# A two-layer graph network: the table stage's weights loaded beside the experts' last steps, and the score products behind a branch

## The chip, the cores and the metric

The kernel runs on one core of one Trainium2 chip. The metric is the device time of one execution in microseconds (us), and the time of a kernel is the median of several runs.

## The reference

A graph has 3125 nodes of 256 features, 100,000 edges and eight types of edge. Two layers follow one another. Each adds to the node features x three things: a message-passing network over the edges, a linear attention over all nodes, and a mixture of experts of which each node uses two. What matters here, cut from the reference (`act` stands for the exact gelu, `ln` for a normalization without weights):

```python
# layer 0, the experts: E = 8, hidden size 1024
logits = xt @ Wr + br
top_p, top_idx = jax.lax.top_k(softmax(logits), 2)
h = act(einsum('end,edh->enh', ln(xt) * ln_g + ln_b, W1) + b1)
y = einsum('enh,ehd->end', h, W2) + b2
x = x + (weights * y_of_the_two).sum(axis=1)
...
# layer 1, the network over the edges: R = 8 types, 8 heads of 32
xn = ln(x)
h_all = einsum('nf,rof->rno', xn, W)                 # a table of R * N rows
scores = einsum('ehd,hd->eh', h_all[type, src], attn_src) \
       + einsum('ehd,hd->eh', h_all[type, dst], attn_dst)
...
# layer 1, the attention: keys and values
k, v = ln_k(heads(xn @ wk.T)), ln_v(heads(xn @ wv.T))
kv = einsum('bhsd,bhse->bhde', k, v) / N
```

The scores are linear in h_all, so the kernel multiplies the attention vectors into the weights once: a small matrix `score_w` (256 rows, 2 × 8 × 8 columns) gives both halves of every score from xn itself.

## The kernel before, in words

The work is one program, `fast` (line 2117), whose stages follow one another. The nodes lie in 25 tiles of 128.

**Layer 0** up to line 2277: adjacency, linear attention, two rounds of aggregation, then the router (`tokens`, its logits added at line 1901) and the plan that scatters each node's rows to the experts (`plan`, scatters of rows at line 1951).

**The experts** (`experts`, line 2017) make 30 steps of 256 rows, s = 0 to 29. `fetch(s + 1)` at the head of step s issues seven loads on the SP queue: the rows fx (line 2036), four small ones (2040 to 2043), and the two halves of the expert's weights, fw1 and fw2 (2045, 2047), 1 MB each, two buffers each. Then come the first product fhp (2072) with the gelu on ACT (2073), the turn of the next step's rows (ftp, 2056, and fxe, 2058), the second product fyp (2080), the bias (2082), the store of the rows (2083, on ACT's queue), and `beside(s)` (2282), which does a share of other work. In the experts `tc.manual_schedule(engines=ORDERED)` holds: TensorE (PE), VectorE (DVE) and ScalarE (ACT) execute in written order, whereas SP and GpSimd (POOL) are placed by the scheduler.

In `beside`, step 16 loads the layer-1 weights wn on POOL's queue (line 2286, 8 loads of 256 KB). At step 22 it calls `score_weights` (2087): six small DVE operations build at_w (2092, 2098), 32 products of wn with at_w go to TensorE (sp, line 2106; each float32 product is two records, so 64), and four DVE copies (2109, 2111) bring them to score_w. After step 29 a branch (`tc.If`, 2311) holds two seldom steps more. It isn't taken with these inputs.

**The table stage** (2318 to 2411) is scheduled freely on all engines. Ahead of its loop are the loads of its weights on SP: wq, wo (line 353 in `load_k`), wt (2 MB), wkv, bo, kg and kb (2330 to 2337), and a row of padding (2339 to 2341). For each node tile t it gathers two rows y per node from the experts' output (POOL, 2351; three buffers each), adds them to xs (DVE, 2354), takes mean and variance (2356, 2357), a square root on ACT and a reciprocal (2358, 2359), normalizes to x (338), and turns it: tp on TensorE (345), copied to xt on ACT (346). From xt come four products hp of 128 × 512 columns with wt (2371; 16 records), copied to the table's stage by ACT for even j (2376) and by DVE for odd j (2374); the scores ap (2379, 2380) with score_w; and kvp (2389), whose normalization (2392 to 2405) leads to kv (2408). The two PSUM buffers of hp are used in turn, so product j + 2 waits for the copy of product j.

**Layer 1** (`Layer1`, line 1145) then walks over the edges by blocks: gathers of table rows (r, line 1404) and sums (line 1493). Its order is written out by hand.

Pools of SBUF tiles are stacks of addresses. A tile that lies where another lay before waits for the last use of that one. Loads and stores issued on SP and ACT signal through eight semaphores in rotation, so an issue waits for the landing of the transfer eight before it.

Of the kernel before, what the change touches and what calls it, by code (L numbers as in the profile page):

```python
# [8 lines left out]
F32 = mybir.dt.float32  # L9
BF = mybir.dt.bfloat16  # L10
I32 = mybir.dt.int32
AF = mybir.ActivationFunctionType
OP = mybir.AluOpType
# [2002 lines left out]

def experts(tc, C, T, a, pool, wp, wk, ps, beside, first, steps):
# [69 lines left out]
def score_weights(nc, C, a, late, f, wn, blk_p):  # L2087
# [6 lines left out]
    for i, name in enumerate(("L1_gnn_attn_srcc", "L1_gnn_attn_dstc")):  # L2094
        col = f.tile([P, 2], F32, name=f"att{i}")
        nc.sync.dma_start(col, a[name])
        for oc in range(2):
            nc.vector.tensor_scalar(at_w[:, oc, i * HD:(i + 1) * HD], head[:, oc, :],
                                    col[:, oc:oc + 1], None, op0=OP.mult)

# [16 lines left out]
def fast(ctx: ExitStack, tc: tile.TileContext, a, out, flag):  # L2117
# [153 lines left out]


    with tc.tile_pool(name="blk", bufs=1) as blk, tc.tile_pool(name="blk_p", bufs=1, space=PSUM) as blk_p, \
            tc.tile_pool(name="f", bufs=1) as f:
        B_ = Blocks(nc, late, dram, blk, a, places)

        score_w = None
        wn = f.tile([P, R, 2, D], F32, name="wn")
# [3 lines left out]
        def beside(s):  # L2282
            nonlocal score_w
            if s == 16:
                for r in range(R):
                    tc.keep_in_program_order(nc.gpsimd.dma_start(
                        wn[:, r], a["L1_gnn_W"][r].rearrange("(k p) n -> p k n", p=P)))
            if s == 22:
                score_w = score_weights(nc, C, a, late, f, wn, blk_p)
# [17 lines left out]
        with tc.tile_pool(name="fw", bufs=2) as fw, tc.tile_pool(name="fk", bufs=3) as fk, \  # L2307
                tc.tile_pool(name="fp", bufs=2, space=PSUM) as fp:
            with tc.manual_schedule(engines=ORDERED):
                experts(tc, C, T_, a, f, fw, fk, fp, beside, 0, NE0 + NT - SELDOM)  # L2310
        with tc.If(nc.values_load(T_.over[0:1, 0:1], min_val=0, max_val=1) > 0):
            with tc.tile_pool(name="fw_l", bufs=2) as fw, tc.tile_pool(name="fk_l", bufs=3) as fk, \
                    tc.tile_pool(name="fp_l", bufs=2, space=PSUM) as fp:
                with tc.manual_schedule(engines=ORDERED):
                    experts(tc, C, T_, a, f, fw, fk, fp, lambda s: None, NE0 + NT - SELDOM, NE0 + NT)


    with tc.tile_pool(name="n1", bufs=1) as n1:
        apart = dram.tile([NB, P, 3, HD * R], BF, name="apart")
        x1t = dram.tile([(NB + 3) // 4, P, 2, 512], F32, name="x1t")  # L2320
        cx = n1.tile([P, 2, P], F32, name="cx1")
        wq = load_k(nc, n1, a["L1_mix_wqT"], "wq")
        wo = load_k(nc, n1, a["L1_mix_woT"], "wo")
        with tc.tile_pool(name="r", bufs=1) as r1, tc.tile_pool(name="rw", bufs=3) as rw, \
                tc.tile_pool(name="rc", bufs=1, space=PSUM) as rc, \
                tc.tile_pool(name="rp", bufs=2, space=PSUM) as rp:
            wt = load_k(nc, r1, a["L1_gnn_WT"], "wt")
            wkv = r1.tile([P, 2, 2 * D], F32, name="wkv")
            for i, name in enumerate(("L1_mix_wkT", "L1_mix_wvT")):
                nc.sync.dma_start(wkv[:, :, i * D:(i + 1) * D], a[name].rearrange("(k p) n -> p k n", p=P))  # L2330
            bo = r1.tile([P, D], F32, name="bo")
            nc.sync.dma_start(bo, row_bc(a["L1_mix_bo"], D))
            kg = r1.tile([P, 2, 64], F32, name="kg")
            kb = r1.tile([P, 2, 64], F32, name="kb")
            for i, c in enumerate("kv"):
                nc.sync.dma_start(kg[:, i, :], row_bc(a[f"L1_mix_ln_{c}_g"], 64))
                nc.sync.dma_start(kb[:, i, :], row_bc(a[f"L1_mix_ln_{c}_b"], 64))
            pad = r1.tile([1, TW], F32, name="pad")
            nc.vector.memset(pad[:, :D], 0.0)
            nc.vector.memset(pad[:, D:], FAR)  # L2340
            nc.sync.dma_start(tab2[PADTAB:PADTAB + 1, :], pad)

            st = r1.tile([P, NB, 6], F32, name="st_x2")
            mv = r1.tile([P, NB, 2], F32, name="mv_x2")
            rs = r1.tile([P, NB], F32, name="rs_x2")
            cps = [rc.tile([P, P], F32, name=f"kv{g}") for g in range(2)]
            rows = tab2[:R * NP, :].rearrange("(r t p) c -> t p r c", r=R, p=P)
            for t in range(NB):
                for i in range(2):
                    y = rw.tile([P, D], F32, name=f"y{i}")  # L2350
                    nc.gpsimd.indirect_dma_start(  # L2351
                        out=y, out_offset=None, in_=T_.y,
                        in_offset=bass.IndirectOffsetOnAxis(ap=T_.back[:, i * NB + t:i * NB + t + 1], axis=0))
                    nc.vector.scalar_tensor_tensor(xs[:, t, :], y, T_.wt[:, i, t:t + 1], xs[:, t, :],
                                                   op0=OP.mult, op1=OP.add)
                nc.vector.bn_stats(st[:, t, :], xs[:, t, :])
                nc.vector.bn_aggr(mv[:, t, :], st[:, t, :])
                nc.scalar.activation(rs[:, t:t + 1], mv[:, t, 1:2], AF.Sqrt, bias=C.eps)
                nc.vector.reciprocal(rs[:, t:t + 1], rs[:, t:t + 1])
                x1 = rw.tile([P, D], F32, name="x1")  # L2360
                normal(nc, x1, xs[:, t, :], mv, rs, t)
                nc.vector.tensor_add(xs[:, t, :], xs[:, t, :], bo)
                xt = rw.tile([P, 2, P], F32, name="xt1")
                transposed(nc, C, rp, xt, x1)
                nc.sync.dma_start(x1t[t // 4][:, :, t % 4 * P:(t % 4 + 1) * P], xt)

                stage = rw.tile([P, R, TW], F32, name="stage")
                for j in range(R // 2):
                    hp = rp.tile([P, 2, D], F32, name="hp", tag="a")
                    for k in range(2):  # L2370
                        nc.tensor.matmul(hp.rearrange("p r d -> p (r d)"), xt[:, k, :],  # L2371
                                         wt[:, k, j * 512:(j + 1) * 512], start=(k == 0), stop=(k == 1))
                    if j % 2:
                        nc.vector.tensor_copy(stage[:, 2 * j:2 * j + 2, :D], hp)
                    else:
                        nc.scalar.copy(stage[:, 2 * j:2 * j + 2, :D], hp)
                ap = rp.tile([P, 2 * R * HD], F32, name="ap", tag="b")
                for k in range(2):
                    nc.tensor.matmul(ap, xt[:, k, :], score_w[:, k, :], start=(k == 0), stop=(k == 1))
                nc.vector.tensor_copy(stage[:, :, D:], ap[:, :R * HD].rearrange("p (r h) -> p r h", r=R))  # L2380
                a3 = rw.tile([P, 3, HD * R], BF, name="a3")
                bf_parts(nc, rw, a3[:, 0, :], a3[:, 1, :], a3[:, 2, :], ap[:, R * HD:], [P, HD * R])
                nc.sync.dma_start(apart[t], a3)
                nc.sync.dma_start(rows[t], stage)

                n = P if t < NB - 1 else LAST
                kvp = rp.tile([P, 8, 64], F32, name="kvp", tag="b")
                for k in range(2):
                    nc.tensor.matmul(kvp.rearrange("p h d -> p (h d)"), xt[:, k, :], wkv[:, k, :],  # L2389
                                     start=(k == 0), stop=(k == 1))  # L2390
                mean = rw.tile([P, 8], F32, name="mean")
                nc.vector.tensor_reduce(mean, kvp, AX.X, OP.add)
                nc.vector.tensor_scalar(mean, mean, 1.0 / 64, None, op0=OP.mult)
                kv = rw.tile([P, 8, 64], F32, name="kv")
                nc.vector.tensor_tensor(kv, kvp, mean[:, :, None].to_broadcast([P, 8, 64]), OP.subtract)
                sq = rw.tile([P, 8, 64], F32, name="sq")
                nc.scalar.activation(sq, kv, AF.Square)
                var = rw.tile([P, 8], F32, name="var")
                nc.vector.tensor_reduce(var, sq, AX.X, OP.add)
                nc.scalar.activation(var, var, AF.Sqrt, bias=C.eps, scale=1.0 / 64)  # L2400
                nc.vector.reciprocal(var, var)
                nc.vector.tensor_tensor(kv, kv, var[:, :, None].to_broadcast([P, 8, 64]), OP.mult)
                kv4 = kv.rearrange("p (i h) d -> p i h d", i=2)
                nc.vector.tensor_tensor(kv4, kv4, kg[:, :, None, :].to_broadcast([P, 2, 4, 64]), OP.mult)
# [75 lines left out]
```

## Time and profile before

| what | value |
| --- | --- |
| three runs, us | 3027.10, 3026.31, 3028.59 (median 3027.1) |
| the profiled execution | 3027.1 us, of which its span on the core 3025.3 |
| mean granted TensorE clock | 0.916 of full speed |
| busy share of the span | PE 83%, DVE 61%, POOL 33%, ACT 24% |
| moved by DMA | 416.82 MB, mean 138 GB/s |
| step of the experts away from `beside`'s larger shares | 14.31 us |
| table stage, first gather to last kv | 1377.6 to 1653.5 us |

The span runs from the first instruction to the last. In lines of the profile, PE is TensorE's matmuls and PEld its weight loads, which overlap them. A line of the timeline has the start and the length of a run of equal instructions, then engine, source line, operation, output <- inputs, shape and count; the bracket tells how long the engine sat idle before and what ended it. "SPq" and "ACTq" are instructions that issue transfers. In a row of windows, each engine has its busy time in the stretch and, in brackets, its number of instructions. The granted clock is the share of full speed that TensorE was given.

### The profile page before, as it was taken

To read this page: it belongs to the slowest core of one execution; us is meant where nothing else is said; L and a number is where in the kernel's file an instruction comes from. 1 tells how busy PE (TensorE), PEld (TensorE's weight loads), DVE (VectorE), ACT (ScalarE), POOL (GpSimd) and SP (SyncE) were. 2 spreads that over 40 slices of the span, in tenths; PEclk is the share of its full clock that TensorE was granted. 3 is DMA by queue.
4 is the path that set the end of the run, shared out by engine and by line. 5 is a ranking of instruction groups with operands and counts; after the bars stand their busy time and mean duration, and the time that the engine had idled before them with its cause. 6 is when DMAs were issued, how large, how long until landed. Compare 5 with 4: busy or idle time off the path is not lost.

```text
span 3025.3 us, 37763 instructions
## 1 busy us (share of the span) xinstructions
PE 2522.7 (83%) x13349; PEld 1720.9 (57%) x13349; DVE 1842.2 (61%) x4082; ACT 735.1 (24%) x1646; POOL 997.2 (33%) x1040
## 2 busy tenths in 40 slices
PE   2788799999978999997998565977877977969788
PEld 1556554455557888883444444555555654655556
DVE  7999787756562111116866577657667766676652
ACT  3444212222232222222322111212121212112122
POOL 2000000002224600005101777765747656666500
PEclk9899999999988999898999777998989887988999
DMA  3333356533334666455434555544535445455412
GB/s 111 73 73 76 105 185 210 190 95 109 93 118 153 225 196 198 147 171 181 152 124 140 161 139 152 152 139 129 166 100 160 142 119 150 132 148 142 121 42 89
DMA packets 383645, 416.82 MB, mean 138 GB/s; under 512 B 143189, under 2 KB 318298, under 8 KB 383188
## 3 DMA queue, kind: packets, MB, share of 16 engines
q1 hardware_dynamic: 313454, 266.28, 28.9%
q0 software_dynamic: 49072, 132.49, 15.5%
q10 hardware_dynamic: 20918, 15.51, 1.7%
q8 instruction: 109, 1.79, 0.2%
q14 instruction: 92, 0.75, 0.1%
HBM read 316.18 MB, written 97.96 MB: 137 GB/s over the span
## 4 chain that ended last, share of the span: by engine, by line
PE 29%; DVE 9%; POOL 6%; DMA 5%; issue 4%; ACT 2%; DVEq 0%; ACTq 0%; SPq 0%; POOLq 0%
PE sums L1493 8%; PE hp L1285 7%; POOL r L1404 6%; PE hp L2371 5%; PE yp L1337 4%; DMA r<-tab,b_at 3%; DVE r L1479 1%; PE kvp L2389 1%; DVE oh L1482 1%; PE dp L1229 1%; PE yp L1596 1%; DMA y<-route_y,slot 1%; DMA ew<-in_L_ffn_expert_w 1%; DVE xs L1341 1%; ACT h L1288 0%
## 5 line engine op out<-in xcount | busy, mean ns | idle before, releaser
L1404 POOL DMA_INDIRECT r<-tab,b_at x831 | 801.4, 964 | 603.0 <-issue 228.5
L1493 PE MATMUL sums<-r,oh 128*128 128x264 f32 x1662 | 417.5, 407 | 46.6 <-DVE oh L1482 24.2
L1493 PEld LDWEIGHTS sums<-r,oh 128*128 128x128 f32 x1662 | 330.0, 201 | 127.4 <-issue 30.3
L1951 POOL DMA_INDIRECT route_x<-x,slot x50 | 50.6, 1012 | 811.9 <-DVE slot L1947 644.2
L1479 DVE TENSOR_TENSOR r<-r,fixed 128x1792 f32<-128x1792 f32 (+2 forms) x123 | 239.5, 1947 | 3.4 <-ACT fixed L1467 3.4
L2072 PE MATMUL fhp<-fxe,fw 128*128 128x256 f32 x960 | 219.5, 387 | 0.9 <-DVE fxe L2058 0.6
L2222 PE MATMUL agg<-at,px 128*128 128x512 bf16 (+2 forms) x1050 | 217.2, 358 | 2.2 <-DMA row_g<-in_L_gnn_g 2.2
L1337 PE MATMUL yp<-ew,h 128*128 128x256 f32 x600 | 162.3, 422 | 66.8 <-DVE xs L1341 59.7
L2222 PE MATMUL agg<-at,py 128*128 128x512 bf16 (+4 forms) x1200 | 217.9, 335 | 0.0
L1288 ACT ACTIVATE h<-hp,bc 128x512 f32<-128x512 f32 (+2 forms) x168 | 106.2, 639 | 450.5 <-PE hp L1285 450.5
L2080 PE MATMUL fyp<-fw,fhid 128*128 128x256 f32 x960 | 212.2, 379 | 0.0
L2072 PEld LDWEIGHTS fhp<-fxe,fw 128*128 128x128 f32 x960 | 176.3, 193 | 38.6 <-ACT fhid L2073 6.6
L2080 PEld LDWEIGHTS fyp<-fw,fhid 128*128 128x128 f32 x960 | 180.3, 190 | 23.2
L1285 PE MATMUL hp<-xt,ew 128*128 128x512 f32 (+2 forms) x336 | 166.7, 624 | 22.1 <-ACT h L1288 13.0
L2371 PE MATMUL hp<-wt,xt 128*128 128x512 f32 x400 | 180.7, 601 | 3.2 <-ACT xt L346 2.7
L1229 PE MATMUL dp<-a,ot 128*128 128x64 bf16 x2493 | 111.2, 208 | 85.5 <-DVE own L1240 43.8
L1337 PEld LDWEIGHTS yp<-ew,h 128*128 128x128 f32 x600 | 122.5, 212 | 101.8 <-DVE xs L1341 66.7
L2073 ACT ACTIVATE fhid<-fhp,fb 128x256 f32<-128x256 f32 x240 | 113.5, 473 | 270.7 <-PE fhp L2072 254.8
L1229 PEld LDWEIGHTS <-ot 128*128 128x128 bf16 x2493 | 106.2, 108 | 108.7 <-issue 50.3
L2351 POOL DMA_INDIRECT y<-route_y,slot x50 | 51.2, 1025 | 350.4 <-DVE pad L2340 325.3
L2222 PEld LDWEIGHTS <-py 128*128 128x128 bf16 (+1 forms) x1200 | 111.5, 99 | 88.1 <-issue 5.5
L2222 PEld LDWEIGHTS <-px 128*128 128x128 bf16 (+1 forms) x1050 | 96.3, 98 | 105.4 <-issue 10.3
(423 smaller groups left out, 3841.3 us busy)
## 6 DMA issues: line engine op xcount, KB each, us to landing
fw<-in_L_ffn_W SPq DMA_DIRECT2D x60, 1024.0 KB
ew<-in_L_ffn_expert_w SPq DMA_DIRECT2D x126, 256.0 KB
at<-adj SPq DMA_DIRECT2D x44, 640.0 KB
route_x<-zero SPq DMA_DIRECT2D x104, 256.0 KB
tab<-stage SPq DMA_DIRECT2D x25, 1056.0 KB
oe<-b_order SPq DMA_DIRECT2D x97, 256.0 KB
adj<-adj_o SPq DMA_DIRECT2D x78, 250.0 KB
r<-tab,b_at POOLq DMA_INDIRECT x831
```

The source lines that it names most:

```text
L1229: nc.tensor.matmul(dp[:, i, :, :].rearrange("p h r -> p (h r)"), ot[:, i * P:(i + 1) * P], A["a3"][:, j, :], start=(j == 0), stop=(j == 2))
L1285: nc.tensor.matmul(hp[:, :W], ws[i, e][:, n, j * P:(j + 1) * P], x[:, n, :W], start=(n == 0), stop=(n == 1))
L1288: nc.scalar.activation(o[:, j, :W], hp[:, :W], AF.Relu, bias=b[:, e, j:j + 1])
L1337: nc.tensor.matmul(yp, h2[e][:, n, i * P:(i + 1) * P], ws[3, e][:, n, :], start=(n == 0), stop=(n == 1))
L1404: st = self.nc.gpsimd.indirect_dma_start(out=r[:, c, :], out_offset=None, in_=self.table, in_offset=bass.IndirectOffsetOnAxis(ap=self.B.at ...
L1479: nc.vector.tensor_tensor(rv, rv, self.factors[:, s0:s0 + k, :, None].to_broadcast([P, k, HD, DH]), OP.mult)
L1493: mm = nc.tensor.matmul(self.sums, oh[:, c, :], r[:, c, :], start=(i == 0), stop=(i == w - 1))
L2072: nc.tensor.matmul(hp, w1[:, k, i * P:(i + 1) * P], xe[:, k, :], start=(k == 0), stop=(k == 1))
L2073: nc.scalar.activation(hid[:, i, :], hp, AF.Gelu, bias=b1[:, 0, i:i + 1])
L2080: nc.tensor.matmul(yp, hid[:, i, t * P:(t + 1) * P], w2[:, i, :], start=(i == 0), stop=(i == K1 - 1))
L2222: nc.tensor.matmul(agg[g][:, :cw], parts[j][:n, k, g * P:(g + 1) * P], at[:n, i, :cw], start=(k == 0 and j == 0), stop=(k == NB - 1 and j ...
L2371: nc.tensor.matmul(hp.rearrange("p r d -> p (r d)"), xt[:, k, :], wt[:, k, j * 512:(j + 1) * 512], start=(k == 0), stop=(k == 1))
```

## The change

A new function `table_weights` makes the tiles of the table stage's weights in pools that are opened before the experts, and a generator of six portions of loads on SP. `beside` draws one portion at each step from 24 on: a quarter of wt (512 KB) at steps 24 to 27; wkv and bo at 28; kg, kb, wq and wo at 29. `score_weights` is split: `score_columns` builds at_w at step 22, and the products and copies stand after the branch. wn and at_w move to a pool that lives until the table stage ends. A square root of one column, `root`, stands on ACT at the experts' end. The rest of the table stage keeps its text, with one level of indentation less.

```diff
+def table_weights(tc, a, n1, r1):
+    nc = tc.nc
+    wq, wo = (n1.tile([P, 2, D], F32, name=n) for n in ("wq", "wo"))
+    wt = r1.tile([P, 2, R * D], F32, name="wt")
+    wkv = r1.tile([P, 2, 2 * D], F32, name="wkv")
+    bo = r1.tile([P, D], F32, name="bo")
+    kg, kb = (r1.tile([P, 2, 64], F32, name=n) for n in ("kg", "kb"))
+    def loads():
+        split = lambda name: a[name].rearrange("(k p) n -> p k n", p=P)
+        keep = lambda o, i: tc.keep_in_program_order(nc.sync.dma_start(o, i))
+        for x in range(0, R * D, 512):
+            keep(wt[:, :, x:x + 512], split("L1_gnn_WT")[:, :, x:x + 512])
+            yield
+        for i, name in enumerate(("L1_mix_wkT", "L1_mix_wvT")):
+            keep(wkv[:, :, i * D:(i + 1) * D], split(name))
+        keep(bo, row_bc(a["L1_mix_bo"], D))
+        yield
+        for i, c in enumerate("kv"):
+            keep(kg[:, i, :], row_bc(a[f"L1_mix_ln_{c}_g"], 64))
+            keep(kb[:, i, :], row_bc(a[f"L1_mix_ln_{c}_b"], 64))
+        keep(wq, split("L1_mix_wqT"))
+        keep(wo, split("L1_mix_woT"))
+        yield
+    return (wq, wo, wt, wkv, bo, kg, kb), loads()
...
-def score_weights(nc, C, a, late, f, wn, blk_p):
+def score_columns(nc, C, a, f):
...
+    return at_w
+
+def score_weights(nc, at_w, late, wn, blk_p):
...
+    n1 = ctx.enter_context(tc.tile_pool(name="n1", bufs=1))
+    table_hold = ExitStack()
+    r1 = table_hold.enter_context(tc.tile_pool(name="r", bufs=1))
...
-        score_w = None
-        wn = f.tile([P, R, 2, D], F32, name="wn")
+        ready = table_weights(tc, a, n1, r1)
+        at_w = None
+        wn = r1.tile([P, R, 2, D], F32, name="wn")
...
+            if s >= 24:
+                next(ready[1], None)
             if s == 22:
-                score_w = score_weights(nc, C, a, late, f, wn, blk_p)
+                at_w = score_columns(nc, C, a, r1)
...
                 experts(tc, C, T_, a, f, fw, fk, fp, beside, 0, NE0 + NT - SELDOM)
+                nc.scalar.activation(r1.tile([P, 1], F32, name="root"), C.eps, AF.Sqrt)
         with tc.If(nc.values_load(T_.over[0:1, 0:1], min_val=0, max_val=1) > 0):
...
+        score_w = score_weights(nc, at_w, late, wn, blk_p)
...
-        wq = load_k(nc, n1, a["L1_mix_wqT"], "wq")
-        wo = load_k(nc, n1, a["L1_mix_woT"], "wo")
...
-            wt = load_k(nc, r1, a["L1_gnn_WT"], "wt")
...
+    wq, wo, wt, wkv, bo, kg, kb = ready[0]
```

## The prediction

> **What bounds the kernel now.** I read the page first, then the windows by stage, and the timeline and the chain of waits only where the change touches. On the page one line places both ends of the change:
>
> ```profile
> L2371 PE MATMUL hp<-wt,xt 128*128 128x512 f32 x400 | 180.7, 601 | 3.2 <-ACT xt L346 2.7
> ```
>
> TensorE waited only 3.2 us ahead of the table stage's 400 hp records, so that stage is bound by TensorE once it runs, and a late start is carried to its end. The experts, from the timeline (start, length, engine, line, count, and in brackets the wait before and its releaser):
>
> ```profile
> 1240.95 7.12 PE L2072 MATMUL fhp<-fxe,fw 128*128 128x256 f32 x32
> ...
> 1256.60 13.02 PE L2106 MATMUL sp<-at_w,wn 128*128 128x16 f32 x64 [1.19 <-DVE at_w L2098]
> 1269.46 9.68 PE L2072 MATMUL fhp<-fxe,fw 128*128 128x256 f32 x32
> ...
> 1286.32 3.88 PE L2072 MATMUL fhp<-fxe,fw 128*128 128x256 f32 x17
> ```
>
> An undisturbed step takes 14.31 us (fhp starts at 1343.54 and 1357.85). Here three fhp starts in a row lie 28.51 and 16.86 us apart. The windows (length, then busy time of PE, PEld, DVE, ACT and POOL, clock, DMA share, GB/s) say how:
>
> ```profile
> 1256.60:1269.60 13.00, 13.00 (x65) 13.00 (x65) 0.08 (x1) 0.00 (x0) 0.00 (x0) 0.54 0.44 131
> 1269.60:1276.00 6.40, 6.40 (x20) 5.18 (x20) 1.58 (x6) 1.69 (x4) 0.00 (x0) 0.61 0.01 3
> ...
> 1304.00:1347.00 43.00, 43.00 (x206) 36.90 (x205) 6.11 (x19) 11.36 (x24) 0.00 (x0) 1.00 0.60 194
> 1375.00:1393.00 18.00, 0.09 (x2) 0.10 (x2) 5.77 (x20) 1.87 (x3) 11.44 (x12) 0.56 0.74 254
> ```
>
> The products hold TensorE alone for 13.0 us at a granted clock of 0.54, and the clock is still 0.61 in the next 6.4 us. The last row is the second place: after the branch TensorE does nothing for some 18 us. What it waits for is in the timeline:
>
> ```profile
> 1377.63 1.01 POOL L2351 DMA_INDIRECT y<-route_y,slot  x1 [325.31 <-DVE pad L2340]
> ...
> 1381.59 0.48 DVE L2354 SCALAR_TENSOR_TENSOR xs<-y,route_w,xs 128x256 f32<-128x256 f32 x1 [4.86 <-DMA y<-route_y,slot]
> ...
> 1392.93 1.09 PE L345 MATMUL tp<-ident,x 128*128 128x128 f32 x4 [17.91 <-DMA kb<-in_L_mix_ln_k_b]
> ...
> 1396.83 9.05 PE L2371 MATMUL hp<-wt,xt 128*128 128x512 f32 x16
> ```
>
> The first gather lands 3.96 us after its issue, before the weights' transfers are under way; those issued beside them land late, as the chain of waits shows:
>
> ```profile
> 1380.24 7.15 DMA y<-route_y,slot
> ...
> 1388.17 6.84 DMA y<-route_y,slot
> ```
>
> **The change, part by part.**
>
> 1. *Products leave step 22.* (28.51 + 16.86) − 2 × 14.31 = 16.75 us: 13.0 of products, 1.2 of waiting for at_w, 2.55 of fhp at the low clock (9.68 against 7.12). TensorE is busy throughout in the steps around it (43.00 of 43.00), so the following steps move up by all of it. The six at_w operations stay; nothing on TensorE waits for them there. **−16.75.**
>
> 2. *Weights loaded beside steps 24 to 29.* About 3.4 MB more go out on SP: four chunks of wt of 0.5 MB behind steps 24 to 27, wkv and bo behind 28, the rest behind 29. On SP a chunk stands behind the next step's second weight half and ahead of the following step's fx. Each weight half of the experts (1 MB) is issued when its buffer of two steps ago is done, so it has 2 × 14.31 − 7.1 = 21.5 us until its use. A step moves 194 GB/s × 14.31 us = 2.8 MB; a chunk makes that 3.3 MB, or 231 GB/s, where this trace sustains 345 GB/s (890 to 903 us, DMA share 0.95). Hidden: **0**. Without that cover it is 3.4 MB at 345 GB/s, 10 us. The eight loads that went out after the branch (issues 1378.02 to 1384.92) are gone from SP there; TensorE's 17.91 us end with one of them only by the record, x being ready just then at 1392.9.
>
> 3. *Start of the experts.* The longer-lived pools push the weight buffers onto addresses last read by the router (pr, done 902.84), so the first four weight loads, issued at 889.7 to 891.3 now, go out at about 902.9. At 345 GB/s their 4.2 MB end near 915; the first half lands by 906, well before fhp at 922.08. But the last scatter of rows (issued 911.5) now lands beside them, and fx (917.62) waits for it. A gather beside loads took 7.1 instead of 3.96 us, so 0 to +3.2; I take **+1.0**, since the loads cover at most the first 3.6 of the scatter's 6.1 us. The small first-step loads move behind fx, to about 920.7, where the first fxe needs them at 921.4.
>
> 4. *Start of the table stage.* In the new order TensorE has the 64 products first, then tp(0), hp(0), ap(0), kvp(0), tp(1), tp(2), hp(1). From the branch at 1376.4 (old times): products 13.0 (clock low after the pause, as in the row above) to 1389.4; DVE's four copies 0.67 (1269.66 to 1270.33), to 1390.1. Written behind them on DVE: xs five times, the two statistics operations of tile 0, its reciprocal and its x, nine operations that start about 0.38 apart in the rows at 1389.91 to 1391.87: to 1393.5. tp(0) and the copy to xt took 1.15 (1392.93 to 1394.07), so hp(0) starts at 1394.7, **2.1 us earlier** than 1396.83. But ap(0) (0.45) and tp(1) and tp(2) (0.9 together), done ahead of hp(0) before, are still to come. And here is the added wait: the copies wait for sp, behind them in DVE's order stand all xs, and behind those POOL's gathers, which from tile 3 on wait for xs of tile 0, 1 and so on to free a buffer. For tile 3 that is at 1390.65 instead of 1385.23, so at POOL's 1.25 us per gather tile 6's first one goes at 1398.1 and lands at 1402.1, even at 4.0 us. DVE's order puts that tile's xs ahead of its copy of stage(0, j=1), for which the fourth quarter of hp(0) waits: stall 1.4 us. hp(1) then starts at about 1408.1 (1407.43 before). The next such copies, written behind tiles 7 and 8, cost 1.7 in hp(1) by the same stepping. So −2.1 + 0.45 + 0.9 + 1.4 + 1.7 = **+2.4**, and hp(3) at 1430.5 instead of 1428.14, after which the ten microseconds per tile are TensorE's again. Ends: −2.1 if the earlier hp(0) is kept; +8.6 if all that lay between the first xs and hp(0) (1396.83 − 1381.59 = 15.2) repeats from 1390.1. I take the stepped value, which lies between them.
>
> 5. *The root activation on ACT.* The table load of 1.28 us (1388.06) goes ahead of the branch, but the reciprocal it led to ran only at 1391.87, held by DVE's order. **0**, at most −1.3. The pad's store moved ahead of the experts: 0.
>
> Sum: −16.75 + 0 + 1.0 + 2.4 = −13.35. The profiled execution took 3027.1 us (span 3025.3 and 1.8 around it), which is the median too (3026.31 to 3028.59): **3013.7 us**.
>
> Two rules against these rows. On the clock: sp ran 13 us without a pause at 0.54, and fhp behind it was slow too. The Trainium skill, "TensorE: Matmul & The Clock Gate", Part 1: The HAM clock gate, says that about 3.4 us of sustained work releases the throttle; by it the products after the branch would need some 8 us (an estimate) and hp would start warm, about 5 + 2 us better than my sum. The row of this very operation contradicts it, and decides. On the loads: the Trainium skill, "DMA: Bandwidth & Descriptors", Queues, rings and completion order, says that a DMA engine serves its queues in turn, packet by packet. That speaks against part 2, since wt chunks take turns with the stores and row loads of the steps; with 21.5 us of slack I leave it at 0.
>
> **The rivals.**
>
> *The start loses nothing.* hp(0) is 2.1 us early and DVE catches up before a copy stalls TensorE: −16.75 + 1.0 − 2.1 = −17.85, **3009.3**. For it: gathers land in 4 us without loads beside them. Against: the later gathers start 5.4 us later, and DVE was busy 10.00 of 10.00 us from 1407 to 1417 already.
>
> *The products are only moved.* They stand ahead of a DVE that works in order, and its backlog is as long as before: −16.75 + 1.0 + 8.6 + 1.4 = −5.75, **3021.4**, which is no change. For it: the copies are written ahead of every xs. Against: 12.2 us of DVE's 18 (1375 to 1393) were idle, and six gathers will lie ready.
>
> *Slower: the loads are not hidden.* If the DMA engines can't carry the steps and the chunks together, TensorE waits for fw in steps 25 to 29, and 3.4 MB cost 3.4 MB over the rate: at 131 GB/s (the window of sp) 26 us, −13.35 + 26 = +12.6, **3039.7**. It decides below 175 GB/s, from where it eats 13.35 + 6.05. For it: share 0.60 already. Against: 345 GB/s at 890.
>
> **How the numbers follow.** About 0.2% (6.05 us) can be told from no change, so faster means below 3021.0 and slower above 3033.2. My forecast (3010.5 to 3018) 0.50; nothing lost (below 3010.5) 0.20; only moved (above 3018) 0.25, half of it below 3021.0; not hidden 0.05. Faster 0.50 + 0.20 + 0.13 = 0.83, same 0.12, slower 0.05. Range: low, 3009.3 less the scatter's 1.0 and the table load's 1.3, 3007, and 1 below for products at a better clock; high, 3021.4. **3006 to 3022**.
>
> **What would show it.** Step 22 at 14.31 us with no sp; fhp in 24 to 29 without a wait for fw; 64 sp records of 13 us after the branch at clock 0.5; gathers landing in 4 us; hp(3) 54 us after the branch (1430.5 − 1376.4), 52 before; the first fhp within 3 us of 922. The forecast is wrong if fhp waits for fw, if sp there takes 8 us, or if stage copies stall more than two tiles.

## The result, and the profile after

The changed kernel took 3019.2 us (median of 12 runs, 3010.7 to 3030.2) and the one before 3026.7 us (12 runs, 3018.4 to 3039.3): a ratio of 0.9976, 95% interval 0.9959 to 0.9993, so 2 to 12 us less. Ten more runs against 33 of before gave 0.9960 (0.9941 to 0.9979). The profiled execution took 3014.1 us, its span 3012.3 (before 3025.3). In two later groups of runs every kernel, the one before too, took some 500 us more; what those runs are good for is said where they come.

The changed places, from the timeline of the changed kernel:

```profile
1247.91 7.12 PE L2101 MATMUL fhp<-fxe,fw 128*128 128x256 f32 x32
...
1262.21 7.12 PE L2101 MATMUL fhp<-fxe,fw 128*128 128x256 f32 x32
...
1366.77 13.81 PE L2140 MATMUL sp<-at_w,wn 128*128 128x16 f32 x64 [1.15 <-PEq L2354]
1384.65 0.66 PE L345 MATMUL tp<-ident,x 128*128 128x128 f32 x2 [4.08 <-issue]
1386.17 7.25 PE L2401 MATMUL hp<-wt,xt 128*128 128x512 f32 x12 [0.86 <-ACT xt L346]
1393.94 1.98 PE L2401 MATMUL hp<-wt,xt 128*128 128x512 f32 x4 [0.52 <-DVE stage L2404]
...
1400.90 7.13 PE L2401 MATMUL hp<-wt,xt 128*128 128x512 f32 x16 [2.38 <-ACT xt L346]
```

The step of 28.5 us is gone: two fhp starts lie 14.30 apart. The products stand behind the branch and take 13.81 us there (13.02 before). Behind them TensorE waits 4.08 us for x of tile 0, and hp(1) waits 2.38 us for its xt. The windows of the changed kernel (columns as in the prediction):

```profile
1290.90:1305.30 14.40, 14.40 (x70) 12.28 (x69) 3.44 (x7) 3.79 (x8) 0.00 (x0) 1.00 0.70 229
1310.00:1353.00 43.00, 43.00 (x205) 36.76 (x204) 6.32 (x20) 11.30 (x24) 0.00 (x0) 1.00 0.66 212
1366.70:1380.60 13.90, 13.81 (x64) 13.73 (x64) 0.00 (x0) 0.00 (x0) 5.78 (x6) 0.50 0.21 58
```

With a chunk a step moves 229 GB/s (first row, step 25) where it moved 194, close to the 231 of the prediction, and TensorE is still busy in all of the time, also over the 43 us of the second row. Under the products DVE and ACT do nothing at all: 0.00 and 0.00.

To compare kernels I cut each profile at the same instructions: the router's last pr (line 1901), the first fhp, tot (the last small product of `beside(29)`), hp(n) (the products of node tile n in the table stage), and its last kv. A row that bears a label in place of a name is a variant that is described below. The times are starts of TensorE's weight loads (for pr, of the operation on DVE), in us:

| kernel | pr to first fhp | first fhp to tot | tot to hp(0) | to hp(1) | to hp(3) | to last kv | ratio to before (95%) |
| --- | --- | --- | --- | --- | --- | --- | --- |
| before | 19.4 | 452.7 | 21.9 | 32.3 | 53.4 | 278.5 | |
| changed | 20.8 | 435.8 | 20.8 | 35.5 | 56.0 | 280.9 | 0.9976 (0.9959 to 0.9993) |
| changed, again | 20.8 | 436.8 | 20.8 | 35.2 | 56.0 | 280.9 | 0.9960 (0.9941 to 0.9979) |
| products_only | 20.9 | 436.2 | 20.4 | 35.5 | 56.4 | 281.4 | 0.9963 (0.9947 to 0.9979) |
| loads_only | 20.8 | 451.9 | 12.7 | 28.2 | 49.9 | 274.8 | 0.9995 (0.9977 to 1.0013) |
| no_products | 20.7 | 436.6 | 12.8 | 27.8 | 48.8 | 273.8 | 0.9947 (0.9929 to 0.9965) |
| copies_late_3 | 21.7 | 435.8 | 16.3 | 28.7 | 48.7 | 273.6 | 0.9954 (0.9935 to 0.9973) |

From pr to the last kv the changed kernel is 1.4 − 16.9 + 2.4 = −13.1 us against before (−12.2 in its second profile). The rest of the program varies from execution to execution: pr lies at 902.7 us before and at 908.8, 897.3, 908.4, 909.8, 899.6 and 911.0 in the other six profiles of the table, which up to there do the same work, and from the last kv to the end it is 1366 to 1375 us. One cause is in the windows of layer 0, first before, then changed:

```profile
190.00:336.00 146.00, 119.97 (x1030) 87.84 (x1029) 135.71 (x192) 67.60 (x160) 0.00 (x0) 0.99 0.34 76
```

```profile
190.00:336.00 146.00, 122.21 (x966) 89.04 (x966) 129.09 (x184) 64.74 (x153) 0.00 (x0) 0.93 0.32 72
```

The granted clock was 0.99 and 0.93 there, and TensorE got through 1030 and 966 instructions of the same list. The seven profiles of the table fall into two groups by this window: the three at 0.99 have pr at 897 to 903 us, the four at 0.93 at 908 to 911. The same changed kernel is once in each group.

### The profile page after: what moved, and what is told of

It reads as the page before. It is cut to its first block, busy times and chain, and to the rows that moved or that the text cites. A ratio compares the mean times of both kernels' runs of the same rounds, so it can differ in the third digit from the quotient of the medians.

```text
span 3012.3 us, 37730 instructions
## 1 busy us (share of the span) xinstructions
PE 2511.8 (83%) x13307; PEld 1717.5 (57%) x13349; DVE 1841.0 (61%) x4082; ACT 737.1 (24%) x1648; POOL 995.9 (33%) x1040
## 4 chain that ended last, share of the span: by engine, by line
PE 29%; DVE 9%; POOL 6%; DMA 5%; issue 4%; ACT 2%; SPq 0%; DVEq 0%; ACTq 0%; POOLq 0%
PE sums L1493 8%; PE hp L1285 6%; POOL r L1404 6%; PE hp L2401 5%; PE yp L1337 4%; DMA r<-tab,b_at 3%; DVE r L1479 1%; PE kvp L2419 1%; DMA ew<-in_L_ffn_expert_w 1%; DVE oh L1482 1%; PE dp L1229 1%; PE yp L1596 1%; DVE xs L1341 1%; PE sp L2140 0%; PE yb L1356 0%
## 5 line engine op out<-in xcount | busy, mean ns | idle before, releaser
L2256 PE MATMUL agg<-at,py 128*128 128x512 bf16 (+5 forms) x1181 | 214.1, 332 | 0.9
L1285 PE MATMUL hp<-xt,ew 128*128 128x512 f32 (+2 forms) x336 | 162.8, 611 | 22.8 <-ACT h L1288 13.4
```

Of the source, the lines that this page charges most:

```text
L1285: nc.tensor.matmul(hp[:, :W], ws[i, e][:, n, j * P:(j + 1) * P], x[:, n, :W], start=(n == 0), stop=(n == 1))
L2256: nc.tensor.matmul(agg[g][:, :cw], parts[j][:n, k, g * P:(g + 1) * P], at[:n, i, :cw], start=(k == 0 and j == 0), stop=(k == NB - 1 and j ...
```

## The experiments

**The changed kernel again.** No edit.

> The changed kernel once more. Theory: what the change does is done in three places and repeats: 13.4 us from the first of the weight loads being due to the first fhp instead of the plan's old order (first fhp about 1.2 us later behind the router's last pr than before), 30 experts' steps 16.9 us shorter, and hp(3) 55.9 us after tot (53.3 before); sum -13. The 7 us by which the changed kernel's profile was behind at the router are chance, so pr falls elsewhere this time, within some 6 us of 905. Rival: the new order delays layer 0 as well, pr again comes 6 us or more after the 902.7 of before, and the gain over the whole is 7 us, ratio 0.9975.

(The 13.4 in it is a slip; the sum goes by the 1.2.) All three places repeat within 1.0 us, two of them within 0.1. pr came at 897.3, earlier than in the kernel before, with the clock of 0.99 in layer 0. So the 6 us by which the first profile was late there don't come with the new order each time, and the rival falls in that form. A smaller shift of the average isn't excluded, since there is one profile of the kernel before.

**Each part alone.** First the products behind the branch with the weights loaded after it:

```diff
-            if s >= 24:
-                next(ready[1], None)
...
         score_w = score_weights(nc, at_w, late, wn, blk_p)
+    run_all(ready[1])
```

> The products moved behind the branch, the table stage's weights loaded after the branch again (same tiles, same addresses). Theory: the products fill the time in which TensorE waited for the gathers, and the loads have 13.8 us of them to hide behind, so the early loads add little: hp(3) 55.9 us after tot, give or take 1.5, and a time like the changed kernel's, 13 us below before. Rival: the early loads carry the gain; with the loads beside the gathers these land after 7 us, hp(3) comes 60 us or more after tot and the gain is 9 us or less.

The last kv came at 281.4, 0.4 later than with the early loads, while the steps 24 to 28 are back at 14.30 instead of 14.38. From pr to the last kv this version takes 738.4 us, the changed kernel 737.5 and 738.4: the early loads add at most 1 us to this change. Then the loads alone:

```diff
-                at_w = score_columns(nc, C, a, r1)
+                at_w = score_weights(nc, score_columns(nc, C, a, r1), late, wn, blk_p)
...
-        score_w = score_weights(nc, at_w, late, wn, blk_p)
+        score_w = at_w
```

> The early loads alone, the products back in step 22. Theory: step 22 keeps its 16.75 us; behind the branch the gathers land in 4 us, x(0) is ready 12.3 us after tot and hp(0) starts at 13.7 (22.0 before), hp(3) at about 45 (53.3): +1.2 -8.3 = -7 us against before. So the two parts alone give 13 and 7, and together 13, not 20. Rival: DVE's backlog takes the lead back, hp(3) at 50 or later, and the loads alone give 2 us or nothing.

hp(0) came at 12.7, even earlier than the theory had it, but more than half of the lead of 9.2 us is gone by hp(1), and 3.7 us are left at the last kv. The size was wrong and the rival nearly right: hp(3) at 49.9, a ratio of 0.9995. From hp(0) to hp(1) it takes 15.5 us, where the kernel before takes 10.4. DVE waits for gathers there (waits of DVE, 1386 to 1416 us: total, times, longest):

```profile
DVE xs L2384 <- DMA y<-route_y,slot: 11.5, 10, 4.9
```

Of these, 7.5 us lie ahead of hp(0), where TensorE waits as well, and 4.0 us behind it, most of them in front of the copies that hp(0) and xt of tile 1 need. From hp(0) to hp(1) the changed kernel has 3.7 us of such waits and the kernel before none. The first six gathers of the changed kernel ran under the products, so its xs find them ready. Early loads and moved products thus work on the same idle time: alone they gain 3.1 and 12.2 us from pr to the last kv; together, in the two profiles of the changed kernel, 13.1 and 12.2, and not 15.3.

**The products left out** (the copies too):

```diff
-        score_w = score_weights(nc, at_w, late, wn, blk_p)
+        score_w = late.tile([P, 2, 2 * R * HD], F32, name="score_w")
+        nc.vector.memset(score_w, 0.0)
```

> Leaves out the products and their copies: score_w is set to zero, so the scores are wrong. Bounds what the products cost where they stand now. Theory: hp(0) at 13.7 us after tot and hp(3) at 45 as with the loads alone, step 22 at 14.31: -16.9 + 1.2 - 8.3 = -24 us against before, so the products cost 11 of their 13.8 us behind the branch. Rival: the gathers and DVE's backlog set the pace there and the products lie in their shadow: hp(3) at 53 or later and a time within 3 us of the changed kernel.

The last kv comes 7.1 us earlier than in the changed kernel. So the products, with their copies, cost 7.1 us behind the branch, though they take 13.8 there; leaving step 22 gained 16.9. That is between the two expectations: hp(0) came at 12.8, as the theory had it or earlier, hp(3) at 48.8 and neither at 45 nor at 53.

**Where the 7.1 us come from.** DVE's four copies wait for the products, and all xs stand behind them; or TensorE's own time is the cost. The copies are put behind x of tile 0:

```diff
-        score_w = score_weights(nc, at_w, late, wn, blk_p)
...
+        score_w, sp = score_weights(nc, at_w, late, wn, rp)
...
+            if t == 0:
+                one = r1.tile([P, 1], F32, name="one")
+                nc.vector.tensor_scalar(one, x1[:, 0:1], 0.0, 1.0, op0=OP.mult, op1=OP.add)
+                score_copies(nc, score_w, sp, one)
```

> The changed kernel, with DVE's four copies to score_w behind x of tile 0 instead of ahead of every xs (they multiply by a one that is made from x of tile 0, so that the order is forced; the values are the same). Theory: what the products cost behind the branch is DVE's wait for them, not TensorE's time: tile 0 is added and normalized under the products, hp(0) starts at 16.3 us after tot (20.8), the gathers from tile 3 on go 6 us earlier, and the last kv comes 5 us earlier, at 275.5 to 276 after tot (280.9). Rival: TensorE's 13.8 us are the cost; then only hp(0) moves, and the last kv stays within 1.5 us of 280.9.

Beside it went eight buffers for each gathered tile, both edits at once, and a filler in the kernel before:

```diff
-                y = rw.tile([P, D], F32, name=f"y{i}")
+                y = rw.tile([P, D], F32, name=f"y{i}", bufs=8)
```

> The changed kernel, with eight buffers for each of the two gathered tiles instead of three, so that 16 gathers instead of 6 need no wait for DVE. Theory: between hp(0) and hp(1) the changed kernel loses 4 us (14.7 instead of 10.4) because DVE's written order waits for gathers that waited for DVE; with the gathers ahead, hp(0) stays at 20.8 after tot, hp(1) comes at about 31.5 (35.5), and the last kv at 277 (280.9). Rival: DVE's own backlog of work is what holds hp(1), and nothing moves by more than 1 us.

> Both: eight buffers and the late copies. Theory: hp(0) at 16.3 after tot, hp(1) 10.4 to 11 behind it, the last kv at about 273 (280.9), so 8 us below the changed kernel, 20 below before. Rival: the two take away the same wait, and the last kv is that of the better of the two alone, 275.5 or later.

```diff
+        nc.gpsimd.memset(f.tile([P, 7424], F32, name="shift")[:, :1], 0.0)
```

> The kernel before, with an unused tile of 29,696 bytes that moves the experts' weight buffers to the addresses that the changed kernel gives them. Theory: the first four weight loads go out behind the router's last pr, and the experts' first rows are read 1.4 us later behind the last scatter (7.5 instead of 6.1 us), with all else as before: step 22 at 28.6, hp(3) 53.4 after tot. Rival: the delay of 1.4 us comes from the small loads or the padding's store that the change moved; then it stays at 6.1 here.

In this group of runs the kernel before took 3533.1 us, the late copies 3529.3 (ratio 0.9960, 0.9926 to 0.9994), eight buffers 3556.8 (1.0066, 1.0028 to 1.0105) and both 3545.5 (1.0031, 0.9997 to 1.0065). The theory's times did not come: hp(0) at 20.2, 27.9 and 34.1 after tot, the last kv at 288.8, 296.1 and 297.5. The timeline of the late copies shows why it could not be asked here:

```profile
1400.87 0.67 PE L345 MATMUL tp<-ident,x 128*128 128x128 f32 x2
...
1405.41 0.28 DVE L2146 TENSOR_SCALAR score_w<-sp,one 128x64 f32<-128x64 f32 x1 [7.43 <-remote]
1405.50 0.37 ACT L346 COPY xt<-tp 128x256 f32<-128x256 f32 x1 [11.14 <-remote]
```

By its records TensorE had done sp by 1401.0 and tp by 1401.6, and the two engines that wait for them went on only at 1405.4 and 1405.5; the last gather of the train was issued at 1401.95. The profile of the repetition below has the same two waits (7.48 and 11.18 us). The kernel with the filler is the kernel before but for addresses, and it answers its own question even under this condition: the rows fx are read 7.3 us behind the last scatter's issue (6.1 before, 7.5 changed). Its first weight load goes out at 913.26, just behind pr at 913.06. So most of the delay, 1.2 of 1.4 us, is that of the moved weight buffers. The rest of its theory, all else as before, did not hold here: step 22 took 27.3 us, and hp(3) came 56.8 after tot.

**The same three on another chip**, then the late copies a third time, on a third chip:

> The late copies once more, on another chip: on the last one every kernel, the one before too, took some 500 us more, and other engines stood waiting for TensorE where nothing in the trace held it (DVE from 1397.9 to 1405.4 in this kernel, with sp at its end by 1401.0). Theory: hp(0) at 16.3 us after tot (20.8), the last kv at 275.5 to 276 (280.9). Rival: TensorE's 13.8 us are the cost; the last kv within 1.5 us of 280.9.

> Eight buffers for each gathered tile, on another chip. Theory: hp(0) at 20.8 after tot, hp(1) at about 31.5 (35.5), the last kv at 277 (280.9). Rival: DVE's own backlog holds hp(1), and nothing moves by more than 1 us.

> Both edits, on another chip. Theory: hp(0) at 16.3 after tot, hp(1) 10.4 to 11 behind it, the last kv at about 273 (280.9): 8 us below the changed kernel, 20 below before (ratio 0.9935). Rival: the two take away the same wait, and the last kv is that of the better of the two alone, 275.5 or later.

It was the chip of the first four experiments, where before had taken 3029.7 us, and it now took 3550.8: no property of a chip. hp(0) again at 20.2, 27.9 and 34.2; ratios 0.9977 (0.9952 to 1.0001), 1.0025 (1.0001 to 1.0048) and 1.0032 (1.0004 to 1.0060). Eight buffers are only known under this condition, where hp(0) came later with them (27.9 and 34.2 instead of 20.2). What they do otherwise stays open.

> The late copies a third time, since in the two runs so far TensorE's results reached the other engines late wherever a train of gathers was being issued, in the kernel before as well (some 500 us over all), and that hides what is asked. If that is gone: theory, DVE's wait for the products is what they cost behind the branch: hp(0) at 16.3 us after tot (20.8), hp(1) 4 us or more earlier than 35.5, the last kv at 275.5 to 276 (280.9); rival, TensorE's 13.8 us are the cost and the last kv stays within 1.5 us of 280.9. If it is not gone, hp(0) comes at 20.2 again and the last kv at 286 to 289.

This time before took 3028.2 us and the late copies 3013.7 (2996.9 to 3023.2), ratio 0.9954 (0.9935 to 0.9973). Its timeline (tot at 1368.5):

```profile
1370.01 13.80 PE L2139 MATMUL sp<-at_w,wn 128*128 128x16 f32 x64 [1.25 <-PEq L2356]
...
1374.01 0.48 DVE L2386 SCALAR_TENSOR_TENSOR xs<-y,route_w,xs 128x256 f32<-128x256 f32 x1 [4.91 <-DMA y<-route_y,slot]
...
1378.49 0.95 POOL L2383 DMA_INDIRECT y<-route_y,slot  x1 [0.31 <-issue]
...
1379.16 0.41 DVE L338 TENSOR_SCALAR x<-xs,mv_x,rs_x 128x256 f32<-128x256 f32 x1
...
1383.65 0.67 PE L345 MATMUL tp<-ident,x 128*128 128x128 f32 x2
1383.85 0.28 DVE L2146 TENSOR_SCALAR score_w<-sp,one 128x64 f32<-128x64 f32 x1 [3.11 <-PE sp L2139]
```

x of tile 0 is ready 4.1 us ahead of tp, which follows sp without a gap. The fourth line is the seventh gather, the first that needs a buffer back from xs: it goes out 10.0 us after tot without a wait. In the changed kernel (tot at 1365.4) it went out 16.5 after tot:

```profile
1380.62 0.22 DVE L2143 COPY score_w<-sp 128x64 f32<-128x64 f32 x1 [14.65 <-PE sp L2140]
...
1381.90 1.07 POOL L2381 DMA_INDIRECT y<-route_y,slot  x1 [6.88 <-DVE xs L2384]
```

hp(0) starts at 16.3 as expected, 3.5 later than without the products, but by hp(3) nothing is left of that (48.7 and 48.8), and from hp(0) to hp(1) DVE waits for no gather any more. The last kv comes at 273.6, 7.3 us earlier than in the changed kernel and where it is without any products (273.8). So the 7.1 us are the price of DVE's wait and of the gathers behind it, and TensorE's 13.8 us cost nothing at the last kv. The free schedule of the stage is made anew with each version and is not quite the same: 11 xs stand ahead of DVE's first copy of an hp here, 12 in the changed kernel. What that alone does was not tried. From pr to the last kv this version takes 731.2 us, the changed one 737.5 and 738.4, before 750.6. Over the whole program, its interval and that of the changed kernel overlap, so the times alone do not separate those two.

## Why the prediction was right

Its sum was −13.35; the same stretch measured −13.1 and −12.2. The median of 3019.2 lies in the range, but the medians gained only 7.5 us in the first comparison and 12.8 in the second. What the first lacks is not located: two profiles of the changed kernel agree on the stretch, and outside it single executions differ by more than the gap (pr at 897 to 911). That the profiled execution took 3014.1 us, almost the forecast of 3013.7, is luck: it was 6.1 us late at pr and 6.0 us faster behind the last kv than the kernel before.

1. *Products leave step 22*: forecast −16.75, measured −16.9 and −15.9 for all of the experts. The mechanism and the size hold; the second figure lacks 1.0 in the first step (its two fhp starts lie 17.43 instead of 16.46 us apart), which the change does not touch.
2. *Weights beside steps 24 to 29*: forecast 0. No fhp waited for fw, but steps 24 to 28 take 14.38 instead of 14.30, 0.4 us in all, and 14.30 again where the loads stand behind the branch. Why TensorE is slower beside them stays open.
3. *Start of the experts*: forecast +1.0, measured +1.4, by the chain that was named. The weight loads go out behind pr, and the filler gave most of the same delay:

```profile
908.80 0.17 DVE L1901 TENSOR_TENSOR pr<-lg,br 128x8 f32<-128x8 f32 x1 [0.81 <-PE lg L1898]
...
908.99 0.38 SPq L2074 DMA_DIRECT2D fw<-in_L_ffn_W  x1
```

4. *Start of the table stage*: forecast +2.4, measured +2.4 at the last kv and 2.6 at hp(3). The cause is the one that was named, DVE's wait at the copies; the size of the sum is luck, since its terms were off and cancelled. hp(0) was 1.1 instead of 2.1 us early; its copy stalled it 0.5 instead of 1.4; hp(1) was late by 3.3 instead of 0.7, and what came in between was not in the stepping:

```profile
1397.94 0.48 DVE L2384 SCALAR_TENSOR_TENSOR xs<-y,route_w,xs 128x256 f32<-128x256 f32 x1 [1.94 <-DMA y<-route_y,slot]
...
1399.40 0.21 DVE L2410 COPY stage<-ap 128x64 f32<-128x64 f32 x1
...
1399.65 0.21 ACT L1823 CAST a<-ap 128x64 bf16<-128x64 f32 x1 [3.38 <-DVE stage L2410]
...
1400.50 0.62 ACT L346 COPY xt<-tp 128x256 f32<-128x256 f32 x2
```

DVE's copy of the scores of tile 0 is late behind xs that waited for gathers. ACT's cast waits for it, and xt of tile 1 stands behind the cast. So the lag came through ACT's order, and TensorE waited 2.38 us for xt. The 1.7 us that copies were to cost in hp(1) did not come: its 16 records ran through in 7.13 us, and from hp(1) to hp(3) the changed kernel took 20.4 us where the kernel before took 21.1.

5. *The root activation*: ACT's first square root runs at 1383.12, when it had waited 16.9 us for DVE. `root` did not spare the table load: the one of `root` (1363.37) is followed by another of 1.28 us for line 2388 (1364.97). Both lie ahead of that wait, so 0 holds.

Of the rivals, "the start loses nothing" falls with hp(3) 2.6 us late, "the products are only moved" with a last kv 2.4 and not 8.6 us late, and "the loads are not hidden" with fhp's missing waits. The clock behaved as the row of sp said: 0.50 through 13.9 us. In step 22 of the kernel before, behind steps at full clock, it even was full when the products began, and fell 0.9 us into them:

```profile
1256.60:1257.50 0.90, 0.90 (x8) 0.90 (x9) 0.08 (x1) 0.00 (x0) 0.00 (x0) 1.00 0.62 135
1257.60:1269.60 12.00, 12.00 (x58) 12.00 (x57) 0.00 (x0) 0.00 (x0) 0.00 (x0) 0.50 0.42 131
```

The Trainium skill, "TensorE: Matmul & The Clock Gate", Part 1: The HAM clock gate, has the throttle released after about 3.4 us of sustained work; for these products it is not so in any of the profiles. Behind them hp(0) began at 0.50 and had the full clock after 3.6 us, so that its first 12 records took 7.25 us, where the 16 of hp(1) took 7.13 at 1.00:

```profile
1386.20:1389.80 3.60, 3.60 (x5) 1.54 (x6) 3.60 (x14) 0.59 (x2) 2.99 (x3) 0.50 0.57 146
1389.90:1393.40 3.50, 3.50 (x9) 1.26 (x7) 1.73 (x7) 0.88 (x2) 2.69 (x3) 1.00 0.37 101
```

## What to carry to other kernels

Work that is moved into an engine's idle time was free here only when no other engine's in-order queue waited for it: ask which instruction of another engine consumes it, and put that one behind the work that can go on without it. Two edits that fill the same idle time don't add up; test each alone. Where a program's run-to-run spread is as large as the gain, cut the profiles at common instructions and compare the stretches, which here repeat to 0.1 us in two places and to 1.0 in the third.

## What was not expected of the hardware

In two of the four groups of experiments the programs ran some 500 us longer, and by the records TensorE's results reached the engines that wait for them late in stretches where a train of gathers was being issued. In the filler's profile the row of waits for the own-block operation of layer 1, from 1700 to 2900 us, reads

```profile
DVE own L1240 <- remote: 239.2, 17, 60.1
```

while in the profile of the kernel before this operation waits for dp in that stretch (101.8 us, 35 times, at most 5.9) and has no such row. The steps 2 to 8 of the experts, beside which other gathers run, took 15.4 to 16.2 us instead of 14.3 to 14.6; the steps without gathers were as ever, and layer 0 ended at 903 to 922 us (897 to 911 otherwise). The mean granted clock of these executions was 0.86 instead of 0.92, but it is not the reason in the longer steps: from 960 to 1045 us it was 1.00, with the filler as before. That the gathers cause the lateness is not shown, only that the two came together. The same chip showed it in one group of runs and not in another; what sets it off stays open.
